# A convolution kernel's last stage keeps four row blocks on chip and scatters them to the output

## The chip, the cores and the metric

The kernel runs on one core of one Trainium2 chip. The metric is the device time of one execution in microseconds (us), the median of several executions. A profiled execution leaves a trace of every instruction and every DMA packet, and that is what is read here. Engine names are those of the profile: PE is the matrix engine (its weight loads are listed as PEld), DVE the vector engine, ACT the scalar engine, POOL the GpSimd engine and SP the sync engine, which here only issues transfers.

## The reference

The input x is one picture of 512 x 512 places with 64 channels in float32 (67.1 MB). Two layers follow each other, each adding its result to x:

```
x = x + L0(_gn(x), sequence_mask, ...)   # 0/1 mask over the 512 places; its drawn pattern is data
x = x + L1(_gn(x), w_real, w_imag)       # 12 x 12 Fourier modes, mixed over channels
return x

L0: xn = layer_norm(x)
    left  = (xn @ left_w  + left_b)  * mask * sigmoid(xn @ lgate_w + lgate_b)
    right = (xn @ right_w + right_b) * mask * sigmoid(xn @ rgate_w + rgate_b)
    out   = einsum('bkjd,bkid->bijd', left, right)
    out   = (layer_norm(out) @ out_w + out_b) * sigmoid(xn @ ogate_w + ogate_b)
L1: x_ft  = fft2(x)[:, :, :12, :12]
    out   = real(ifft2(einsum('bcmn,comn->bomn', x_ft, w)))
```

`_gn` is a group norm over the whole picture with 32 groups of 2 channels. So each layer needs statistics of all of its input before it can finish, and the second layer also needs the 12 x 12 low Fourier modes of all of it. The value of a place after the second layer is the value after the first plus an inverse transform of 12 x 12 modes.

## The kernel before

**Ranks.** About half of the 512 mask entries are not zero, and `mask[k] * mask[j]` makes the product of the first layer vanish elsewhere. At its start (L72 to L132) the kernel computes on chip a rank for each row: rows with mask come first. `hot` (L116) marks with ones where the rank of a row equals a slot; a matmul with it turns a table of row numbers and Fourier basis values into rank order (`slot_t`, L120 to L126). From that come `src_i`, the row numbers by rank, used by all gathers of x, and `dst_i` (L819), the ranks by row, used by the gathers of the last stage. The part with few masked rows (`compact`, L622 on) is the one that runs here.

**Stages.** The picture is cut into 16 column tiles of 32 columns (`JC`, `NJ`), and each of these into 4 blocks `b` of 128 rows. A column tile of one row block is 128 partitions x 8 KB, 1 MB; it is called a tile below. (1) to about 202 us: all 64 tiles of x are gathered in rank order, their statistics are taken, and masked entries are kept on chip; `group_norm_affine` (L253 to L280) makes the factors of the first group norm. (2) and (3): projections, then the product per channel. (4) from about 690 us: 8 short units for the product, and from about 800 us 32 units of two tiles each (`units`: column tile `jc`, half of the row blocks). A unit is gathered, gated and added, its group norm statistics and row transform are taken, and it is stored to scratch in DRAM (`store`, L1061, tensors `x1_h`), rows in rank order. A unit lies in one of five places on chip (`x_of`). The last unit pair is column tile 15. (5) the last stage, from about 1500 us: group norm, mixing of the modes over channels (`mixed_ps`, L1298), an inverse transform along columns for 128 columns at a time (`back_columns`, L1316 to L1348, which fills a quarter of `parts`), and then for each tile four matmuls with the row basis `rinv` (L1364), four additions on DVE onto the tile (L1371), and a store to the output (L1372, SP's queue).

**What sets the order in stage 5.** Tiles are handled in the order of `tiles_left`. There are 15 buffers (`AHEAD`). `fetch_rows(i)` gathers tile i from `x1_h` in the original row order by an indirect DMA on POOL's queue (L632) into buffer i mod 15; three are issued during the last units, twelve after them (L1250 to L1256), and each later one after the store of the tile that had the buffer. An instruction that has to wait holds up all that stand behind it on its engine's queue, the DMA issues too. `back_columns(0)` comes before tile 0, and `back_columns(1)`, `(2)` and `(3)` after tiles 4, 20 and 36:

```
for jc in range(NJ):
    for b in range(4):
        ...
        ahead = 4 * jc + b + AHEAD
        if ahead < len(tiles_left):
            fetch_rows(ahead)
        if jc % 4 == 1 and b == 0 and jc // 4 < 3:
            back_columns(jc // 4 + 1, pq, pt, False)
```

Tile names of the profile: `places` is the large region on chip that holds the five unit places, the mode weights and some of the buffers; `lx_t` are the other buffers; `x_h` is `x1_h`; `out_x` is the output.

Of the kernel before, what the change touches and what calls it, by code (L numbers as in the profile page):

```python
# [17 lines left out]
P = 128  # L18
# [11 lines left out]
JC = 32  # L30
NJ = N // JC
K = 2 * P
AHEAD = 15
# [13 lines left out]
def conv_preact_kernel(ctx: ExitStack, tc: tile.TileContext, t: dict):  # L47
# [5 lines left out]
    x1_d = dram.tile([N, N, C], F32, name="x1_d")  # L53
    x1_h = [dram.tile([N, HALF, C], F32, name=f"x1_h{h}") for h in range(2)]
    fwd_d = dram.tile([M2, N, C], F32, name="fwd_d")
    inv_d = dram.tile([M2, N, C], F32, name="inv_d")

    mask_i32 = const.tile([P, 4], I32, name="mask_i32")
    for b in range(4):
        nc.sync.dma_start(mask_i32[:, b : b + 1], t["sequence_mask"][:, b * P : (b + 1) * P].rearrange("o p -> p o"))  # L60

    def load_const(name, shape):
        c = const.tile(shape, F32, name=name)
        nc.scalar.dma_start(c, t[name])
        return c

    ident = load_const("c_ident", [P, P])
    center = load_const("c_center", [P, P])
    avg_p = load_const("c_avg_p", [P, P])
    avg_c = load_const("c_avg_c", [P, P])  # L70
    avg_h = load_const("c_avg_h", [P, 2])
    pick = load_const("c_pick", [P, G])  # L72


# [3 lines left out]
    src_i = const.tile([P, 4, NJ], I32, name="src_i")  # L78
    few_i = const.tile([P, NJ // 2], F32, name="few_i")
    nc.sync.dma_start(few_i, t["c_iota"][:, : NJ // 2])  # L80
    n_i = const.tile([1, 1], I32, name="n_i")
    with tc.tile_pool(name="ix", bufs=1) as xp, tc.tile_pool(
        name="ixp", bufs=1, space=PSUM
    ) as xps, tc.manual_schedule():

        def load_here(name, shape):
            c = xp.tile(shape, F32, name=name)
            nc.sync.dma_start(c, t[name])
# [6 lines left out]
        nc.vector.tensor_copy(table[:, :, 1], mask_i32)  # L95
# [18 lines left out]
        hot = xp.tile([P, 4, N], F32, name="hot")  # L114
        for b in range(4):
            nc.vector.tensor_scalar(hot[:, b, :], iota, rank_p[:, b : b + 1], None, ALU.is_equal)  # L116
        for sb in range(4):
            slot_ps = xps.tile([P, 2 + M2], F32, name="slot_ps", bufs=2)
            for b in range(4):
                nc.tensor.matmul(  # L120
                    slot_ps, hot[:, b, sb * P : (sb + 1) * P], table[:, b, :], start=(b == 0), stop=(b == 3)
                )
            nc.vector.tensor_copy(slot_t[:, sb], slot_ps)
            base = xp.tile([P, 1], F32, name="base", bufs=2)
            nc.vector.tensor_scalar(base, slot_t[:, sb, 0:1], float(NJ), None, ALU.mult)
            nc.vector.tensor_scalar(src_i[:, sb, :], iota[:, :NJ], base, None, ALU.add)  # L126
# [489 lines left out]
    def compact(fc):  # L616
# [31 lines left out]
        with tc.tile_pool(name="xc", bufs=1) as cp:  # L648
            xc = cp.tile([P, K + 1, 2, C], F32, name="xc")
            with tc.tile_pool(name="f1", bufs=1) as sp, tc.tile_pool(name="f1x", bufs=2) as xp, tc.tile_pool(  # L650
# [20 lines left out]
                for jc in range(NJ):  # L671
# [138 lines left out]
        with tc.tile_pool(name="tri", bufs=1) as trp:  # L810
# [3 lines left out]

            dst_i = fc.tile([P, 4, NJ // 2], I32, name="dst_i")
            base = fc.tile([P, 4], F32, name="dst_base")
            nc.vector.tensor_scalar(base, rank_p, float(NJ // 2), None, ALU.mult)
            for b in range(4):
# [49 lines left out]
            with tc.manual_schedule(), tc.tile_pool(name="late", bufs=1) as lp:  # L868
# [16 lines left out]
                def place(i):  # L885
                    return places[:, i * 64 * C : (i + 1) * 64 * C].rearrange("p (n c) -> p n c", c=C)
# [35 lines left out]
                ranked = [h.rearrange("s (k j) c -> (s k) (j c)", k=NJ // 2) for h in x1_h]  # L922
                tiles_left = [(jc, b) for jc in range(NJ) for b in range(4)]
                fetched = {}

                def fetch_rows(i):
                    jc, b = tiles_left[i]
                    fetched[jc, b] = buffers[i % AHEAD]
                    gather(fetched[jc, b].rearrange("p j c -> p (j c)"), ranked[jc // 8], dst_i, b, jc % 8)

# [3 lines left out]
                with tc.tile_pool(name="np_x", bufs=LEAD + 2) as tp, tc.tile_pool(  # L934
# [123 lines left out]
                    def store(k, r):  # L1058
                        jc, half = units[k]
                        b = 2 * half + r  # L1060
                        nc.sync.dma_start(  # L1061
                            x1_h[jc // 8][b * P : (b + 1) * P, (jc % 8) * JC : (jc % 8 + 1) * JC, :].rearrange("p j c -> p (j c)"),
                            x_of(k)[:, r * JC : (r + 1) * JC].rearrange("p j c -> p (j c)"),
                        )
# [59 lines left out]
                    for s in range(-LEAD, total_g + 2 * SIZE):  # L1124
# [115 lines left out]
                with tc.tile_pool(name="lq", bufs=1) as qp, tc.tile_pool(name="lx0", bufs=1) as xp0, tc.tile_pool(  # L1240
# [6 lines left out]
                    for i, xp in enumerate(xps):  # L1247
                        buffers += [xp.tile([P, JC, C], F32, name=f"lx_t{i}_{j}") for j in range((2, 2, 1)[i])]
                        if i > 0:
                            buffers += [place(i - 1)[:, r * JC : (r + 1) * JC] for r in range(2)]  # L1250
                    spare = places[:, 7 * 64 * C - 8 * 2 * MODES * M2 : 7 * 64 * C]
                    buffers += [spare[:, i * JC * C : (i + 1) * JC * C].rearrange("p (n c) -> p n c", c=C) for i in range(2)]
                    for i in range(len(fetched), AHEAD):
                        if i == 8:
                            nc.gpsimd.memset(picks, 0.0)
                        fetch_rows(i)  # L1256
                    pick4 = qp.tile([P, 4], F32, name="pick4")
                    nc.scalar.dma_start(pick4, t["c_pick4"])
# [4 lines left out]
                    with tc.tile_pool(name="sps", bufs=1, space=PSUM) as sps:  # L1263
# [85 lines left out]
                    with tc.tile_pool(name="lpq0", bufs=4, space=PSUM) as pq, tc.tile_pool(  # L1349
                        name="lpt0", bufs=4, space=PSUM  # L1350
                    ) as pt:
                        back_columns(0, pq, pt, True)
                    with tc.tile_pool(name="lpq", bufs=2, space=PSUM) as pq, tc.tile_pool(
                        name="lpt", bufs=2, space=PSUM
                    ) as pt, tc.tile_pool(name="lps", bufs=4, space=PSUM) as pp:
                        for jc in range(NJ):
                            for b in range(4):
                                it = parts[:, jc // 8, (jc % 8) * N : (jc % 8 + 1) * N]
                                xt = fetched.pop((jc, b))
                                group = []  # L1360
                                for g in range(4):
                                    ps = pp.tile([P, JC, 16], F32, name="l_ps")
                                    h = slice(32 * g, 32 * g + M2)
                                    nc.tensor.matmul(  # L1364
                                        ps.rearrange("p j o -> p (j o)"), rinv[h, b, :], it[h],
                                        start=True, stop=True, tile_position=(32 * g, 0),
                                    )
                                    group.append(ps)
                                for g, ps in enumerate(group):
                                    os_ = slice(16 * g, 16 * g + 16)  # L1370
                                    nc.vector.tensor_add(xt[:, :, os_], xt[:, :, os_], ps)  # L1371
                                nc.sync.dma_start(  # L1372
                                    out[0, b * P : (b + 1) * P, jc * JC : (jc + 1) * JC, :].rearrange("i j c -> i (j c)"),
                                    xt.rearrange("p j c -> p (j c)"),
                                )
# [82 lines left out]
```

## Time and profile before

| what | before |
|---|---|
| device time, median of 3 (range) | 1820.17 us (1819.5 to 1820.96) |
| device time of the profiled execution | 1827.94 us |
| span of its trace | 1826.1 us |
| busy: PE, DVE, ACT, POOL | 90%, 78%, 53%, 52% of the span |
| moved by DMA | 467.94 MB, mean 256 GB/s |
| HBM read, written | 278.05 MB, 187.56 MB |

The span runs from the first to the last instruction or landing of the trace; 1.84 us of the device time lie around it. The profiled execution took 7.8 us (0.43%) longer than the median of the others. Busy shares are means over stages with quite different limits. A waiting instruction is listed with what released it, and idle time of an engine counts only where that engine is on the way to the end.

### The profile page before, as it was taken

The page shows a single profiled execution, that of the slowest core. Times are in us where ns is not written, and L with a number is a line of the kernel's source. Part 1 is how long each engine was busy: PE and PEld are TensorE (multiplying, and loading weights), DVE is VectorE, ACT ScalarE, POOL GpSimd, SP SyncE. Part 2 cuts the span into 40 slices and gives each one's busy share as a digit, 9 for nine tenths or more (in the row PEclk, how much of TensorE's full clock was granted, in tenths as well). Part 3 has the DMA queues.
Part 4 walks back from the last instruction along what each step waited for, and adds up shares of the span by engine and source line. Part 5 has one row for each costly group of instructions (what it writes and reads, how often), then busy time and mean ns, then how long its engine had stood idle before and what let it go on. Part 6 is the DMA issues. An engine that isn't in the chain of part 4 may idle for free. (4 is left out here: it accounts for less than half of the span.)

```text
span 1826.1 us, 33612 instructions
## 1 busy us (share of the span) xinstructions
PE 1643.6 (90%) x11414; PEld 1290.0 (71%) x11414; DVE 1422.8 (78%) x2968; ACT 961.5 (53%) x1708; POOL 945.0 (52%) x711
## 2 busy tenths in 40 slices
PE   6779899999899999998999999999999967998772
PEld 5666666665687878897888888888888844665431
DVE  6989777777555547888999999999999996765542
ACT  3565565554222249986777777777777751111000
POOL 3656211111000005788999999999999892211120
PEclk9989899999899999999999999999999986555555
DMA  6999245555655512576866776777668689999999
GB/s 253 386 385 370 102 124 137 137 138 149 203 184 175 183 58 117 197 275 237 274 238 243 258 254 229 252 268 271 241 228 291 218 251 414 423 427 426 427 427 382
DMA packets 189573, 467.94 MB, mean 256 GB/s; under 512 B 34896, under 2 KB 134224, under 8 KB 148432
## 3 DMA queue, kind: packets, MB, share of 16 engines
q1 hardware_dynamic: 158496, 262.21, 42.4%
q0 software_dynamic: 27712, 201.40, 28.7%
q10 hardware_dynamic: 3184, 2.08, 0.4%
q8 instruction: 93, 1.52, 0.3%
q14 instruction: 88, 0.72, 0.1%
HBM read 278.05 MB, written 187.56 MB: 255 GB/s over the span
## 5 line engine op out<-in xcount | busy, mean ns | idle before, releaser
L982 PE MATMUL w_ps<-gate_x,xt_c 128*128 128x128 f32 x2048 | 280.6, 281 | 30.3 <-DVE z_t L1198 24.8
L1045 POOL TENSOR_TENSOR places<-places,z_t 128x1024 f32<-128x1024 f32 x127 | 301.0, 2370 | 8.0
L982 PEld LDWEIGHTS w_ps<-gate_x,xt_c 128*128 128x128 f32 x2048 | 252.5, 194 | 45.5 <-DVE z_t L1198 40.5
L982 PE MATMUL c_ps<-center_x,xt_c 128*128 128x128 f32 x2048 | 277.4, 279 | 1.3 <-ACT xt_c L1011 0.7
L982 PEld LDWEIGHTS c_ps<-center_x,xt_c 128*128 128x128 f32 x2048 | 253.6, 195 | 4.0 <-ACT xt_c L977 2.1
L1364 PE MATMUL l_ps<-places,rinv 24*128 24x512 f32 x512 | 207.8, 1125 | 28.5 <-DVE places L1371 18.5
L1100 DVE BATCH_NORM_STATS2 stats2c<-places 128x6 f32<-128x128 f32 x1024 | 220.6, 279 | 8.0 <-POOL places L1045 8.0
L1015 DVE TENSOR_REDUCE scratch<-sq_c 128x16 f32<-128x1024 f32 x160 | 194.6, 1216 | 29.6 <-ACT sq_c L1010 18.6
L1202 POOL TENSOR_TENSOR z_t<-z_t,bias_row_out 128x1024 f32<-128x1024 f32 x32 | 75.6, 2364 | 248.5 <-DVE z_t L1198 244.4
L1149 ACT ACTIVATE z_t<-z_t 128x1024 f32<-128x1024 f32 x128 | 135.4, 1058 | 129.1 <-DVE z_t L1204 111.5
L972 PE MATMUL t_ps<-c_ident,places 128*128 128x128 f32 x1280 | 200.4, 280 | 1.3 <-DVE places L857 1.3
L1364 PEld LDWEIGHTS l_ps<-places,rinv 24*128 24x128 f32 x512 | 120.5, 303 | 110.9 <-DVE places L1371 57.2
L972 PEld LDWEIGHTS t_ps<-c_ident,places 128*128 128x128 f32 x1280 | 145.7, 142 | 61.6 <-issue 53.9
L977 ACT ACTIVATE xt_c<-t_ps,ab_xc 128x512 f32<-128x512 f32 x256 | 176.0, 688 | 14.7 <-PE t_ps L972 13.6
L1198 DVE TENSOR_TENSOR z_t<-w_ps,rs_n 128x512 f32<-128x512 f32 x256 | 172.1, 672 | 9.8 <-PE w_ps L982 9.7
L1007 ACT ACTIVATE sq_c<-c_ps 128x512 f32<-128x512 f32 x256 | 150.5, 588 | 32.8 <-PE c_ps L982 31.3
L682 DVE BATCH_NORM_STATS2 stats1c<-x_ps 128x6 f32<-128x512 f32 x256 | 156.1, 683 | 11.7 <-PE x_ps L681 11.2
L1204 DVE TENSOR_TENSOR z_t<-z_t,scratch 128x1024 f32<-128x1024 f32 x128 | 156.3, 1221 | 9.9 <-ACT rs_n L1021 3.7
L1041 POOL TENSOR_TENSOR z_t<-z_t,places 128x1024 f32<-128x1024 f32 x64 | 151.5, 2367 | 14.7 <-ACT z_t L1149 14.6
L1041 POOL TENSOR_TENSOR z_t<-z_t,bias_row_out 128x1024 f32<-128x1024 f32 x63 | 149.2, 2368 | 5.7 <-ACT z_t L1149 5.4
L1371 DVE TENSOR_TENSOR places<-places,l_ps 128x512 f32<-128x512 f32 x176 | 109.5, 683 | 54.7 <-DMA places<-x_h,dst_i 43.6
L736 POOL COPY rbc<-rq_out 128x512 f32<-128x512 f32 x64 | 38.3, 613 | 212.4 <-DVE rq_out L209 132.0
(211 smaller groups left out, 2749.1 us busy)
## 6 DMA issues: line engine op xcount, KB each, us to landing
x_h<-places SPq DMA_DIRECT2D x64, 1024.0 KB
out_x<-places SPq DMA_DIRECT2D x44, 1024.0 KB
places<-u_d SPq DMA_DIRECT2D x512, 64.0 KB
out_x<-lx_t SPq DMA_DIRECT2D x20, 1024.0 KB
left_d<-o_c SPq DMA_DIRECT2D x64, 256.0 KB
right_d<-o_c SPq DMA_DIRECT2D x64, 256.0 KB
left_raw<-left_d SPq DMA_DIRECT2D x64, 256.0 KB
right_raw<-right_d SPq DMA_DIRECT2D x64, 256.0 KB
```

The lines of the kernel that those rows point to most:

```text
L682: nc.vector.bn_stats(stats[:, 0, 16 * (jc % quarter) + 4 * r + c, :], ps.rearrange("p i k -> p (i k)"))
L972: nc.tensor.transpose(tps[:, i, :], flat[:, o : o + P], ident)
L977: nc.scalar.activation(xts[s], tps, AF.Identity, bias=ab1[:, 2:3])
L982: nc.tensor.matmul(ps[:, 2 * i : 2 * i + 2, :], xts[s][:, i, :], w, start=True, stop=True)
L1007: nc.scalar.activation(sq, cps, AF.Square)
L1015: nc.vector.tensor_reduce(totals[k % 2][:, 8 * (n - 1) : 8 * (n + 1)], sqs.pop(s // 2), AX.X, ALU.add)
L1041: nc.gpsimd.tensor_mul(zs[k, c], zs[k, c], u)
L1045: nc.gpsimd.tensor_add(xr, xr, zs.pop((k, c)))
L1100: nc.vector.bn_stats(st[k // 4][:, g, k % 4, :], x_of(k)[:, :, 2 * g : 2 * g + 2])
L1198: nc.vector.tensor_mul(z[:, 8 * odd : 8 * odd + 8, :], wps, rs)
L1204: nc.vector.tensor_add(z, z, bias_ps["ogate"].unsqueeze(1).to_broadcast([P, 16, C]))
L1364: nc.tensor.matmul(ps.rearrange("p j o -> p (j o)"), rinv[h, b, :], it[h], start=True, stop=True, tile_position=(32 * g, 0),)
```

## The change

The change has five parts.

1. **Column tile 15 is not stored and not gathered.** Its two units stay where they lie (`place(order[0])`, `place(order[1])`) and become buffers 0 to 3. `tiles_left` begins with its four blocks, so the other 60 tiles follow as tiles 4 to 63, and eleven of them are gathered ahead. `x1_h` becomes three tensors of five column tiles.
2. **Their rows are in rank order.** A row basis in rank order, `rank_inv`, is made on chip: three ACT operations spread `hb` to `by_slot`, four transposes on PE between the variance matmul and the mixing, one ACT copy. The four finished tiles are stored by indirect DMAs on POOL's queue, each row to its own place in the output.
3. **`back_columns` in another order:** (3) first, then (0), (1) and (2) after tiles 0, 10 and 26.
4. **The ranks' chain:** the mask is loaded by one DMA, not four, the tables that the chain needs are issued first and on two queues, and `hot` is made for 128 slots at a time between the matmuls that use it.
5. **Matmuls whose result nobody reads** (`at_work`): four of 128x512 ahead of the first group norm's mean, one ahead of its reciprocal root.

```diff
-x1_h = [dram.tile([N, HALF, C], F32, name=f"x1_h{h}") for h in range(2)]
+x1_h = [dram.tile([N, PART * JC, C], F32, name=f"x1_h{h}") for h in range((NJ - 1) // PART)]
...
-for b in range(4):
-    nc.sync.dma_start(mask_i32[:, b : b + 1], t["sequence_mask"][:, b * P : (b + 1) * P].rearrange("o p -> p o"))
+nc.sync.dma_start(mask_i32, t["sequence_mask"].rearrange("o (b p) -> p (o b)", p=P))
...
-tri = load_here("c_tri", [P, P])
-ones = load_here("c_ones", [P, P])
-iota = load_here("c_iota", [P, N])
-table = load_here("c_table", [P, 4, 2 + M2])
+table = load_here(nc.scalar, "c_table", [P, 4, 2 + M2])
+tri = load_here(nc.sync, "c_tri", [P, P])
+ones = load_here(nc.scalar, "c_ones", [P, P])
+iota = load_here(nc.sync, "c_iota", [P, N])
...
-for b in range(4):
-    nc.vector.tensor_scalar(hot[:, b, :], iota, rank_p[:, b : b + 1], None, ALU.is_equal)
+def mark(sb):
+    for b in range(4):
+        one = slice(sb * P, (sb + 1) * P)
+        nc.vector.tensor_scalar(hot[:, b, one], iota[:, one], rank_p[:, b : b + 1], None, ALU.is_equal)
+mark(0)
 for sb in range(4):
...
+    if sb < 3:
+        mark(sb + 1)
...
-ab1 = group_norm_affine(fc, sets, 2 * stats.shape[2], "xc")
+def at_work(count):
+    ps = pt.tile([P, 4, P], F32, name="x_ps")
+    for _ in range(count):
+        nc.tensor.matmul(ps, ident, flat[:, : 4 * P], start=True, stop=True)
+at_work(4)
+ab1 = group_norm_affine(fc, sets, 2 * stats.shape[2], "xc", with_variance=lambda ab: at_work(1))
...
-buffers = [place(7)[:, JC:], places[:, free : free + JC * C].rearrange("p (n c) -> p n c", c=C)]
+buffers = [place(i)[:, r * JC : (r + 1) * JC] for i in order[:2] for r in range(2)]
+buffers += [place(7)[:, JC:], places[:, free : free + JC * C].rearrange("p (n c) -> p n c", c=C)]
...
-tiles_left = [(jc, b) for jc in range(NJ) for b in range(4)]
-fetched = {}
+tiles_left = [(jc, b) for jc in (NJ - 1, *range(NJ - 1)) for b in range(4)]
+fetched = {(NJ - 1, b): buffers[b] for b in range(4)}
...
-if n == 7 and held(0) and v < last:
+if n == 7 and held(0) and v < last - 1:
     store(v, 0)
-if n == 3 and held(1) and v - 1 < last:
+if n == 3 and held(1) and v - 1 < last - 1:
     store(v - 1, 1)
-if n == 6 and v - 1 == last:
-    for r in range(2):
-        store(last, r)
...
+by_slot = places[:, 7 * 64 * C : 7 * 64 * C + 4 * P].rearrange("p (b g m) -> p b g m", b=4, g=4)
+rank_inv = places[:, 7 * 64 * C + 4 * P : 7 * 64 * C + 8 * P].rearrange("p (b k) -> p b k", b=4)
+for k, factor in enumerate((1.0, -1.0)):
+    nc.scalar.mul(by_slot[:, :, :, k:M2:2], hb[:, :, k:M2:2].unsqueeze(2).to_broadcast([P, 4, 4, MODES]), factor / (N * N))
+nc.scalar.copy(by_slot[:, :, :, M2:], hb[:, :, M2:].unsqueeze(2).to_broadcast([P, 4, 4, 32 - M2]))
...
+turned_b = ps_t.tile([P, 4, P], F32, name="t_ps")
+for b in range(4):
+    nc.tensor.transpose(turned_b[:, b, :], by_slot[:, b].rearrange("p g m -> p (g m)"), ident)
+nc.scalar.copy(rank_inv, turned_b)
...
-back_columns(0, pq, pt, True)
+back_columns(3, pq, pt, True)
...
-for jc in range(NJ):
-    for b in range(4):
+for i, (jc, b) in enumerate(tiles_left):
+        kept = jc == NJ - 1
...
-ps.rearrange("p j o -> p (j o)"), rinv[h, b, :], it[h],
+ps.rearrange("p j o -> p (j o)"), (rank_inv if kept else rinv)[h, b, :], it[h],
...
+if kept:
+    nc.gpsimd.indirect_dma_start(
+        out=out.rearrange("o h (k j) c -> (o h k) (j c)", k=NJ),
+        out_offset=bass.IndirectOffsetOnAxis(ap=src_i[:, b, jc : jc + 1], axis=0),
+        in_=xt.rearrange("p j c -> p (j c)"), in_offset=None,
+    )
+else:
     nc.sync.dma_start(
...
-ahead = 4 * jc + b + AHEAD
+ahead = i + AHEAD
 if ahead < len(tiles_left):
     fetch_rows(ahead)
-if jc % 4 == 1 and b == 0 and jc // 4 < 3:
-    back_columns(jc // 4 + 1, pq, pt, False)
+if i in (0, 10, 26):
+    back_columns(i // 10, pq, pt, False)
```

More of the change, by code (lines that the diff above doesn't have):

```diff
@@ L31 @@
 NJ = N // JC
+PART = 5
 K = 2 * P
@@ L65, in load_const @@
         return c
[L67 to L72, printed above, removed]
     rank_p = const.tile([P, 4], F32, name="rank_p")
@@ L78, in conv_preact_kernel @@
     src_i = const.tile([P, 4, NJ], I32, name="src_i")
-    few_i = const.tile([P, NJ // 2], F32, name="few_i")
-    nc.sync.dma_start(few_i, t["c_iota"][:, : NJ // 2])
+    few_i = const.tile([P, PART], F32, name="few_i")
     n_i = const.tile([1, 1], I32, name="n_i")
@@ L84, in conv_preact_kernel, with load_here @@
     ) as xps, tc.manual_schedule():
-        def load_here(name, shape):
+        def load_here(queue, name, shape):
             c = xp.tile(shape, F32, name=name)
-            nc.sync.dma_start(c, t[name])
+            queue.dma_start(c, t[name])
             return c
-        tri = load_here("c_tri", [P, P])
-        ones = load_here("c_ones", [P, P])
-        iota = load_here("c_iota", [P, N])
-        table = load_here("c_table", [P, 4, 2 + M2])
+        table = load_here(nc.scalar, "c_table", [P, 4, 2 + M2])
+        tri = load_here(nc.sync, "c_tri", [P, P])
+        ones = load_here(nc.scalar, "c_ones", [P, P])
+        iota = load_here(nc.sync, "c_iota", [P, N])
+        ident = load_const("c_ident", [P, P])
+        center = load_const("c_center", [P, P])
+        avg_p = load_const("c_avg_p", [P, P])
+        avg_c = load_const("c_avg_c", [P, P])
+        avg_h = load_const("c_avg_h", [P, 2])
+        pick = load_const("c_pick", [P, G])
+        nc.sync.dma_start(few_i, t["c_iota"][:, :PART])
         nc.vector.tensor_copy(table[:, :, 1], mask_i32)
@@ L813, in compact @@
             tri = places.rearrange("p (j r c) -> p j r c", r=2, c=C)
-            dst_i = fc.tile([P, 4, NJ // 2], I32, name="dst_i")
+            dst_i = fc.tile([P, 4, PART], I32, name="dst_i")
             base = fc.tile([P, 4], F32, name="dst_base")
-            nc.vector.tensor_scalar(base, rank_p, float(NJ // 2), None, ALU.mult)
+            nc.vector.tensor_scalar(base, rank_p, float(PART), None, ALU.mult)
             for b in range(4):
@@ L919, in compact @@
                 free = 3 * 64 * C + C * MODES * MODES
-                buffers = [place(7)[:, JC:], places[:, free : free + JC * C].rearrange("p (n c) -> p n c", c=C)]
+                buffers = [place(i)[:, r * JC : (r + 1) * JC] for i in order[:2] for r in range(2)]
+                buffers += [place(7)[:, JC:], places[:, free : free + JC * C].rearrange("p (n c) -> p n c", c=C)]
                 buffers += [place(2)[:, r * JC : (r + 1) * JC] for r in range(2)]
-                ranked = [h.rearrange("s (k j) c -> (s k) (j c)", k=NJ // 2) for h in x1_h]
-                tiles_left = [(jc, b) for jc in range(NJ) for b in range(4)]
-                fetched = {}
+                ranked = [h.rearrange("s (k j) c -> (s k) (j c)", k=PART) for h in x1_h]
+                tiles_left = [(jc, b) for jc in (NJ - 1, *range(NJ - 1)) for b in range(4)]
+                fetched = {(NJ - 1, b): buffers[b] for b in range(4)}
                 def fetch_rows(i):
@@ L928, in fetch_rows @@
                     fetched[jc, b] = buffers[i % AHEAD]
-                    gather(fetched[jc, b].rearrange("p j c -> p (j c)"), ranked[jc // 8], dst_i, b, jc % 8)
+                    gather(fetched[jc, b].rearrange("p j c -> p (j c)"), ranked[jc // PART], dst_i, b, jc % PART)
                 ends = []
@@ L1061, in store @@
                         nc.sync.dma_start(
-                            x1_h[jc // 8][b * P : (b + 1) * P, (jc % 8) * JC : (jc % 8 + 1) * JC, :].rearrange("p j c -> p (j c)"),
+                            x1_h[jc // PART][b * P : (b + 1) * P, (jc % PART) * JC : (jc % PART + 1) * JC, :].rearrange("p j c -> p (j c)"),
                             x_of(k)[:, r * JC : (r + 1) * JC].rearrange("p j c -> p (j c)"),
@@ L1248, in compact @@
                         buffers += [xp.tile([P, JC, C], F32, name=f"lx_t{i}_{j}") for j in range((2, 2, 1)[i])]
-                        if i > 0:
-                            buffers += [place(i - 1)[:, r * JC : (r + 1) * JC] for r in range(2)]
                     spare = places[:, 7 * 64 * C - 8 * 2 * MODES * M2 : 7 * 64 * C]
@@ L1256, in compact @@
                         fetch_rows(i)
+                    by_slot = places[:, 7 * 64 * C : 7 * 64 * C + 4 * P].rearrange("p (b g m) -> p b g m", b=4, g=4)
+                    rank_inv = places[:, 7 * 64 * C + 4 * P : 7 * 64 * C + 8 * P].rearrange("p (b k) -> p b k", b=4)
+                    for k, factor in enumerate((1.0, -1.0)):
+                        nc.scalar.mul(
+                            by_slot[:, :, :, k:M2:2],
+                            hb[:, :, k:M2:2].unsqueeze(2).to_broadcast([P, 4, 4, MODES]), factor / (N * N),
+                        )
+                    nc.scalar.copy(by_slot[:, :, :, M2:], hb[:, :, M2:].unsqueeze(2).to_broadcast([P, 4, 4, 32 - M2]))
                     pick4 = qp.tile([P, 4], F32, name="pick4")
@@ L1371, in compact @@
                                     nc.vector.tensor_add(xt[:, :, os_], xt[:, :, os_], ps)
[L1372 to L1375, printed above, removed]
-                                ahead = 4 * jc + b + AHEAD
+                                if kept:
[3 more added lines that the diff above has]
+                                        in_=xt.rearrange("p j c -> p (j c)"), in_offset=None,
+                                    )
+                                else:
+                                    nc.sync.dma_start(
+                                        out[0, b * P : (b + 1) * P, jc * JC : (jc + 1) * JC, :].rearrange("i j c -> i (j c)"),
+                                        xt.rearrange("p j c -> p (j c)"),
+                                    )
+                                ahead = i + AHEAD
                                 if ahead < len(tiles_left):
                                     fetch_rows(ahead)
-                                if jc % 4 == 1 and b == 0 and jc // 4 < 3:
-                                    back_columns(jc // 4 + 1, pq, pt, False)
+                                if i in (0, 10, 26):
+                                    back_columns(i // 10, pq, pt, False)
     rows_with_mask = nc.values_load(n_i[0:1, 0:1], min_val=0, max_val=N)
```

## The prediction

> **What bounds the kernel now.** The first thing read was the page's strip of 40 slices:
>
> ```profile
> DMA  6999245555655512576866776777668689999999
> GB/s 253 386 385 370 102 124 137 137 138 149 203 184 175 183 58 117 197 275 237 274 238 243 258 254 229 252 268 271 241 228 291 218 251 414 423 427 426 427 427 382
> ```
>
> DMA is full in slices 2 to 4 (x is gathered) and from slice 34 on. Next, busy time by stretch over the end (columns: length, busy us of PE, PEld, DVE, ACT and POOL, granted PE clock, DMA share, GB/s):
>
> ```profile
> 1479.00:1539.40 60.40, 39.19 (x252) 23.94 (x253) 43.01 (x136) 18.02 (x38) 35.69 (x26) 0.74 1.01 361
> 1539.40:1821.60 282.20, 223.60 (x597) 136.16 (x594) 156.72 (x252) 20.03 (x36) 45.90 (x49) 0.50 1.01 424
> 22.00:195.00 173.00, 142.72 (x1011) 115.28 (x1009) 156.39 (x279) 102.64 (x341) 99.65 (x209) 0.96 0.98 381
> ```
>
> After 1539.4 us DMA at about 426 GB/s is the limit, and the end comes when all bytes are moved. Whether it is also the limit from 1479 to 1539.4 a share of 1.01 cannot tell, so the chain of waits was read there, with the timeline for SP's and POOL's transfers:
>
> ```profile
> 1519.13 6.96 PE mixed_ps L1298 x72
> ...
> 1534.64 1.02 ACT places L1348
> ...
> 1535.70 1.18 PE l_ps L1364 x8
> 1536.88 0.68 DVE places L1371
> ```
> ```profile
> 1539.37 8.88 SPq L1372 DMA_DIRECT2D out_x<-places  x4
> ...
> 1550.82 12.18 SPq L1372 DMA_DIRECT2D out_x<-lx_t  x2
> ```
> ```profile
> 1502.22 0.98 POOL L632 DMA_INDIRECT places<-x_h,dst_i  x1
> 1503.51 0.94 POOL L632 DMA_INDIRECT lx_t<-x_h,dst_i  x1 [0.30 <-issue]
> ...
> 1522.98 0.94 POOL L632 DMA_INDIRECT places<-x_h,dst_i  x1 [2.52 <-DMA lx_t<-x_h,dst_i]
> ...
> 1547.08 0.94 POOL L632 DMA_INDIRECT places<-x_h,dst_i  x1 [22.58 <-DVE places L1371]
> 1549.51 0.94 POOL L632 DMA_INDIRECT places<-x_h,dst_i  x1 [1.49 <-DVE lx_t L1371]
> 1551.93 0.93 POOL L632 DMA_INDIRECT places<-x_h,dst_i  x1 [1.48 <-DMA out_x<-places]
> 1557.45 0.94 POOL L632 DMA_INDIRECT places<-x_h,dst_i  x1 [4.59 <-DMA out_x<-places]
> ```
>
> What to see: from the mode mixing to the first finished tile the chain is PE, ACT and DVE, with no transfer in it. The first output store leaves at 1539.37; call that T0. Until then DMA works ahead (last stores to scratch, 15 gathers), stopping only where buffers run out. So T0 is set by computing, and the end by T0 plus what is left to move.
>
> One tile is 1.0486 MB, at 426 GB/s 2.46 us. Left at T0: 64 - 15 = 49 gathers and 64 stores, 113 x 2.46 = 278.0 us, and about 3.5 us of the last gathers ahead (issued to 1522.98), together 281.5. The stretch above took 282.2. The model holds, and the end is read by it.
>
> The start is a chain of its own:
>
> ```profile
> 7.63 0.17 DVE L95 CAST c_table<-mask_i 128x4 f32<-128x4 int32 x1 [7.63 <-DMA c_table<-in_c_table]
> 10.82 1.68 DVE L116 TENSOR_SCALAR hot<-c_iota,rank_p 128x512 f32<-128x512 f32 x4
> ...
> 14.24 1.08 POOL L632 DMA_INDIRECT xg<-in_x,src_i  x1 [13.78 <-DVE src_i L126]
> ```
>
> Nothing large moves before 14.24, and DMA is 0.98 busy from 22 to 195, so an earlier first gather moves everything after it.
>
> **The change, part by part.**
>
> *Ranks' chain.* DVE begins at 7.63, 2.7 us after the issue of the table (4.94), the last of nine transfers on SP. Now the table is ACT's first (0.75) and the mask SP's first (0.76). 0.75 + 2.7 = 3.5 is the early end; 1.8 us more, what issuing four mask loads took, is the late one, 5.3. I take 4.3: 3.3 us gained. `hot` for 128 slots: each operation shrinks from about 0.45 us to at most the 0.28 us of a 128x128 tensor-scalar on DVE (L806), and the matmuls hide part; 0.3. The later marks run under matmuls (four take about 1.7 us, four marks 1.1); uncovered they would cost 3 x 1.1. Sum **-3.6** (-2.0 to -4.5).
>
> *`at_work`.* Between 199.2 (last transpose) and 203.94 (mean) PE stands idle for DVE, and its clock falls:
>
> ```profile
> 204.00:214.20 10.20, 7.78 (x34) 7.06 (x35) 3.68 (x20) 2.82 (x4) 0.00 (x0) 0.50 0.00 0
> ```
>
> Four matmuls of two records each, 0.43 us apiece (L750's 0.589 for 512 columns against L681's 0.272 for 128 gives 0.83 ns a column), fill 3.4 us of that gap; without the gap they would delay the mean by as much. If the clock stays up, the rounds of `cc_ps` at the start of stage 2, 2.75 us then 1.85, save 0.9 each, three of them: -2.7. If it falls anyway, nothing; should the fifth matmul run into the first transposes, +0.5. I take half, **-1.3**. [...]
>
> *Before T0.* The three small ACT operations come while ACT waits for DVE (from 1511); the four transposes (8 records, about 2 us at the low clock) fall in the nine-step reciprocal root on DVE, 1516.0 to 1518.0, when PE has nothing, and the copy ends by about 1518, needed at 1535. Cost 0; without the cover some 3 us. Four scratch stores and four gathers go, 8 x 2.46 = 19.7 us of DMA. All eight lay before T0, which no transfer sets: gain 0 there. Buffers 0 to 3 now hold the kept tiles, so only eleven gathers can go ahead, and DMA will stand idle before T0.
>
> *After T0.* Left are again 49 gathers and 64 stores (four of them scatters): 113, as before. What remains of the 19.7 us is the 3.5 us backlog: **-3.5**. Against it stand three new waits, all at the front.
>
> (a) `back_columns(0)` now comes after tile 0. The same call after tile 4 before made the next store wait 1562.66 - 1550.82 = 11.8 us where the pitch is 2.85. So tile 1 is done at T0 + 11.8, tile 2 at 14.7, tile 3 at 17.5, tile 4 at 20.4.
>
> (b) On POOL's queue scatter and gather alternate, and each gather (15 to 18) needs the scatter just ahead to have left its buffer. From a store's issue to the gather that waits for it the trace has 1539.37 to 1547.08 = 7.7, then 7.3, 6.9, and 9.5 under more load. I take 7.0, as little else moves then, with 5.0 and 9.5 as ends.
>
> (c) In the changed kernel's list of instructions and waits, the first plain store (tile 4, L1404 there) waits for all four scatters, since these write rows of the output known only at run time. All of SP's stores stand behind it, and gathers 19 on behind those.
>
> By hand from T0: scatter 0 at 0.3, gather 15 at 7.3; scatter 1 at 12.1 (tile 1), gather 16 at 19.1; scatter 2 at 20.3 (1.25 per issue on POOL), behind gather 16 in its queue, 2 us more, so gather 17 at 29.3; scatter 3 at 30.6, landed about 38. First bytes of the plain stores at 39. In these 39 us seven tiles have moved, 17.2 us: **+21.8** idle (with the ends, 15.7 to 29). From there seven finished tiles wait and DMA stays full, also over `back_columns(1)`, now after tile 10.
>
> [...]
>
> *Sum:* -3.6 - 1.3 - 3.5 + 21.8 = +13.4 us. On the profiled execution 1827.94 + 13.4 = 1841.3; its 7.8 us above the median are not the change's, so 1820.2 + 13.4, rounded, **1833**.
>
> **Rivals.**
>
> *Faster: T0 is not the gate.* If computing before T0 secretly hangs on DMA (it is full from 1480), eight transfers less bring T0 forward by up to 19.7 us while the front costs less. For: share 1.01. Against: the chain above. It decides once T0 comes more than 13.4 us earlier; with all 19.7, 1820.2 + 13.4 - 19.7 = 1814. With the front's idle time hidden as well, 1820.2 - 19.7 - 4.9 = 1796.
>
> *The scatter wait costs little.* Should a scatter's turn take some 3 us, the four are over when tile 4 is done; the plain stores' first bytes come at 22, four tiles moved till then, 22 - 9.8 = 12 idle, from the pause of `back_columns(0)` alone: 1820.2 - 8.4 + 12 = 1824. For: nothing else uses DMA then. Against: no turn under 6.9 in the trace.
>
> *No change within 0.2%* (3.6 us, about what a measurement can tell): the start gains its bound, 7.2, and idle time is the least, 15.7: 1820.2 - 7.2 - 3.5 + 15.7 = 1825 is the closest the bounds come; a warm PE clock through `mixed_ps` (3.5 us of 6.96) would make it 1822.
>
> **How the numbers follow.** My forecast 0.66; the cheap wait 0.10, which is still slower; within 0.2% 0.07; faster 0.17. So faster 0.17, same 0.07, slower 0.76. The likeliest case alone spans 1825 to 1844 (idle 15.7 with the best start; idle 29 with the poorest: -2 + 0.5 - 3.5 + 29 = 24). Reaching towards the faster cases, the range is 1815 to 1844.
>
> **What the profile after would show.** Right: the first gather near 10.6; DMA idle from about 20 us before the first scatter, then two or three tenths dark up to the first plain store some 38 us after it; SP waiting there for a POOL transfer; POOL's gathers waiting for `out_x`. Clock 1.00 near 205 if `at_work` works. Wrong: the first l_ps much less than 34 us after the last statistics begin (1501 to 1535.7 now), or plain stores within 25 us of the first scatter.

## The result, and the profile after

The changed kernel takes **1832.45 us** (median of 7 runs, 1827.81 to 1834.90); the kernel before, beside it, 1821.49 us (7 runs, 1819.50 to 1824.37). The ratio is **1.0059** (95% interval 1.0048 to 1.0069): 11 us slower. Forecast were 1833 us and 1815 to 1844. A second comparison gave 1.0044 (1.0031 to 1.0058).

The profiled execution of the changed kernel took 1828.97 us, span 1827.2: low among its own runs, as that of before was high among its (1827.94). The two profiles alone show a difference of 1 us where the medians show 11. So for everything that follows a second profile of each is used as well, taken on one chip (below: *before_again*, *after_again*).

The start, from the timeline of the changed kernel (start, length in us, engine, line, operation, idle time before it and what ended it):

```profile
0.75 0.44 ACTq L80 DMA_DIRECT2D c_table<-in_c_table  x1
3.29 0.17 DVE L94 CAST c_table<-mask_i 128x4 f32<-128x4 int32 x1 [3.29 <-DMA mask_i<-in_sequence_mask]
7.15 1.66 DVE L118 TENSOR_SCALAR hot<-c_iota,rank_p 128x128 f32<-128x128 f32 x8
10.36 1.09 POOL L638 DMA_INDIRECT xg<-in_x,src_i  x1 [9.90 <-DVE hot L118]
```

DVE starts at 3.29 instead of 7.63, and the first gather leaves at 10.36 instead of 14.24.

The last stage, from the timeline too: the start of the last statistics, the first matmuls of a kept tile, then every scatter (L1398) and gather (L638) on POOL's queue, and the first plain stores on SP's.

```profile
1485.84 4.34 DVE L1116 BATCH_NORM_STATS2 stats2c<-places 128x6 f32<-128x128 f32 x22
...
1519.00 2.09 PE L1389 MATMUL l_ps<-places 24*128 24x512 f32 x8 [1.10 <-ACT places L1373]
...
1523.87 1.00 POOL L1398 DMA_INDIRECT out_x<-places,src_i  x1 [22.86 <-DVE places L1396]
...
1530.23 0.96 POOL L638 DMA_INDIRECT places<-x_h,dst_i  x1 [5.36 <-DMA out_x<-places,src_i]
...
1535.18 0.99 POOL L1398 DMA_INDIRECT out_x<-places,src_i  x1 [3.99 <-DVE places L1396]
...
1540.53 0.96 POOL L638 DMA_INDIRECT places<-x_h,dst_i  x1 [4.35 <-DMA out_x<-places,src_i]
...
1541.79 0.98 POOL L1398 DMA_INDIRECT out_x<-places,src_i  x1 [0.30 <-DVE places L1396]
...
1549.99 0.96 POOL L638 DMA_INDIRECT places<-x_h,dst_i  x1 [7.22 <-DMA out_x<-places,src_i]
...
1551.26 0.98 POOL L1398 DMA_INDIRECT out_x<-places,src_i  x1 [0.30 <-issue]
...
1559.58 3.11 SPq L1404 DMA_DIRECT2D out_x<-places  x4
1559.65 0.96 POOL L638 DMA_INDIRECT places<-x_h,dst_i  x1 [7.41 <-DMA out_x<-places,src_i]
```

Every gather here is released by a scatter's landing, and the first plain store, of a tile whose buffer four DVE additions had finished at about 1543.5, leaves only at 1559.58. The view of waits, for SP's queue from 1520 us on (engine, line, what it waited for: total us, times, longest), names the cause:

```profile
SPq L1404 <- DMA out_x<-places: 133.2, 30, 4.9
SPq L1404 <- DMA out_x<-places,src_i: 78.0, 1, 78.0
```

One wait of 78.0 us, for a scatter. It is counted from SP's instruction before, at about 1481.6; for the last 16 us of it a finished tile stood waiting, and four stores leave within 3.11 us behind it. What it costs in transfers stands in the table by stretch (length, busy us of PE, PEld, DVE, ACT and POOL, granted PE clock, DMA share, GB/s):

```profile
1500.00:1512.30 12.30, 7.22 (x78) 3.89 (x77) 5.12 (x21) 0.59 (x1) 1.01 (x3) 0.72 0.98 404
1512.30:1523.87 11.57, 7.81 (x50) 5.56 (x50) 6.14 (x11) 4.92 (x10) 0.00 (x0) 0.65 0.01 6
1523.87:1559.58 35.71, 34.10 (x112) 23.65 (x110) 23.86 (x39) 5.25 (x9) 6.84 (x7) 0.50 0.57 206
1559.58:1822.50 262.92, 196.21 (x483) 112.65 (x480) 132.44 (x214) 13.35 (x24) 43.20 (x46) 0.50 1.01 423
204.00:214.20 10.20, 8.88 (x66) 7.70 (x65) 3.28 (x8) 6.52 (x10) 0.00 (x0) 0.95 0.00 0
```

The eleven gathers ahead are through at 1512.3; for 11.6 us DMA has nothing. Then come 35.7 us in which it moves 206 GB/s, half of the 423 in the row behind. From 1559.58 on it is full to the end. The last row is the stretch of time that had clock 0.50 before: now 0.95. It does not hold quite the same work, since stage 2 begins 3.7 us earlier here (first `cc_ps` at 205.66, before at 209.34).

### The profile page after: what moved, and what is told of

Its sections match the earlier page's. It is cut to its first block, busy times and chain, and to the rows that moved or that the text cites. A ratio compares the mean times of both kernels' runs of the same rounds, so it can differ in the third digit from the quotient of the medians.

```text
span 1827.2 us, 33627 instructions
## 1 busy us (share of the span) xinstructions
PE 1647.5 (90%) x11428; PEld 1283.9 (70%) x11428; DVE 1423.7 (78%) x2980; ACT 962.8 (53%) x1712; POOL 946.5 (52%) x711
## 4 chain that ended last, share of the span: by engine, by line
PE 28%; DVE 17%; DMA 10%; POOL 3%; issue 2%; ACT 2%; SPq 1%; DVEq 0%; ACTq 0%; POOLq 0%
PE w_ps L998 6%; PE c_ps L998 6%; DMA places<-x_h,dst_i 5%; PE l_ps L1389 4%; PE t_ps L988 4%; DVE stats2c L1116 4%; DVE z_t L1214 4%; DVE scratch L1031 4%; PE y_ps L1009 4%; DVE z_t L1220 3%; DMA lx_t<-x_h,dst_i 3%; PE f_ps L1088 2%; POOL z_t L1057 1%; POOL places L1061 1%; DVE places L1396 1%
## 5 line engine op out<-in xcount | busy, mean ns | idle before, releaser
L998 PE MATMUL w_ps<-gate_x,xt_c 128*128 128x128 f32 x2048 | 278.9, 280 | 30.6 <-DVE z_t L1214 29.0
L1389 PEld LDWEIGHTS l_ps<-places,rinv 24*128 24x128 f32 x480 | 116.1, 306 | 119.9 <-DVE places L1396 63.5
L1057 POOL TENSOR_TENSOR z_t<-z_t,places 128x1024 f32<-128x1024 f32 x64 | 151.7, 2370 | 13.6 <-ACT z_t L1165 13.4
```

The costliest lines, as they stand in the source:

```text
L998: nc.tensor.matmul(ps[:, 2 * i : 2 * i + 2, :], xts[s][:, i, :], w, start=True, stop=True)
L1057: nc.gpsimd.tensor_mul(zs[k, c], zs[k, c], u)
L1389: nc.tensor.matmul(ps.rearrange("p j o -> p (j o)"), (rank_inv if kept else rinv)[h, b, :], it[h], start=True, stop=True, tile_position=(3 ...
```

## The experiments

Line numbers differ a little between the kernels below; L1398, L1385 (in *kept*) are the scatters, L638, L637, L633, L632 the gathers. The runs of the kernel before beside these kernels took 1825 to 1826 us, not 1821.5, so ratios are compared, not times. For each kernel's profiled execution four marks are read: when the first output store (or scatter) is issued, **T0**; when the first plain store is; when the last packet of the trace ends; and the **idle time**, the stretch from T0 to that last packet less the bytes moved in it at 426.3 GB/s, its rate where it is full. Packets that load code are left out of both.

| kernel | ratio to before (95% interval) | T0 | first plain store | T0 to last packet | bytes after T0 | idle |
|---|---|---|---|---|---|---|
| before, first profile | 1 | 1539.37 | T0 | 284.9 | 119.5 MB | 4.6 |
| before_again | 1.000 (0.9991 to 1.0009) | 1539.36 | T0 | 286.7 | 118.8 MB | 8.1 |
| after, first profile | 1.0059 (1.0048 to 1.0069) | 1523.87 | T0 + 35.7 | 301.8 | 118.5 MB | 23.9 |
| after_again | 1.0044 (1.0031 to 1.0058) | 1530.47 | T0 + 33.7 | 300.0 | 118.5 MB | 22.0 |
| head | 0.9964 (0.9951 to 0.9976) | 1532.03 | T0 | 285.2 | 120.0 MB | 3.8 |
| kept | 1.0079 (1.0065 to 1.0093) | 1538.54 | T0 + 33.8 | 299.6 | 118.5 MB | 21.7 |
| pause | 1.0056 (1.0043 to 1.0069) | 1529.31 | T0 + 33.2 | 299.6 | 118.5 MB | 21.6 |
| plain | 0.9993 (0.9984 to 1.0001) | 1531.05 | T0 | 290.2 | 118.5 MB | 12.2 |
| group | 1.0035 (1.0021 to 1.0049) | 1532.65 | T0 + 24.9 | 298.3 | 118.5 MB | 20.4 |
| both | 1.0015 (1.0006 to 1.0024) | 1530.42 | T0 + 20.8 | 293.4 | 118.5 MB | 15.5 |
| plain_pause | 0.9975 (0.9963 to 0.9987) | 1529.51 | T0 | 287.5 | 118.5 MB | 9.6 |
| last | 1.006 (1.0042 to 1.0078) | 1527.60 | T0 | 297.6 | 118.5 MB | 19.7 |

The theory was that T0 is set by computing, that parts 4 and 5 bring it forward, and that the scatters' waits after T0 cost more. The main rival: transfers set T0, and the eight that are gone bring it forward.

### head: the kernel before with parts 4 and 5 alone

The edit, cut to its core:

```diff
+nc.sync.dma_start(mask_i32, t["sequence_mask"].rearrange("o (b p) -> p (o b)", p=P))
+table = load_here(nc.scalar, "c_table", [P, 4, 2 + M2])
...
+mark(0)
...
+at_work(4)
+ab1 = group_norm_affine(fc, sets, 2 * stats.shape[2], "xc", with_variance=lambda ab: at_work(1))
```

> The kernel before with parts 4 and 5 alone (the ranks' chain and the matmuls whose result nobody reads); last stage as before. My theory: the first gather leaves at 10.4 instead of 14.24 us, the first group norm's factors and stage 2 gain 1.3 more, nothing else moves: 4 to 6 us less than before, 1821.5 - 5 = 1816.5, and the first output store comes some 5 us earlier too. Rival, the gain is lost on the way (some later stage waits for a transfer that has not moved): within 0.1% of before, 1821.

Measured: 1820.09 us (5 runs) against 1826.11, ratio 0.9964, 6.0 us by the medians. The first gather leaves at 9.73, and the first output store 7.3 us earlier than in either profile of before; the stretch behind it is as long as before (285.2 us). Nothing of the gain is lost on the way, and the time is at the upper end of the 4 to 6 us expected. This kernel is faster than both.

### kept: the changed kernel without parts 4 and 5

```diff
-at_work(4)
-ab1 = group_norm_affine(fc, sets, 2 * stats.shape[2], "xc", with_variance=lambda ab: at_work(1))
+ab1 = group_norm_affine(fc, sets, 2 * stats.shape[2], "xc")
```

The loads, `hot` and the ranks' chain are those of before as well.

> The changed kernel without parts 4 and 5: only the four kept tiles, their row basis and the order of back_columns. My theory: the first scatter leaves when the first output store left before (give or take 2 us), and the tail behind it is longer by 17 to 18 us: 1821.5 + 17 = 1838 (1835 to 1841). Rival, transfers gated the first output: of the 15.5 us by which the first output came earlier in the profile after, only about 5.5 are parts 4 and 5, and the other 10 are the eight transfers that are gone; then this kernel's first scatter comes 10 us earlier and the time is 1821.5 - 10 + 17 = 1828.

Measured: ratio 1.0079, 15.6 us by the medians (1841.74 against 1826.11). Its timeline on POOL's queue:

```profile
1538.54 1.00 POOL L1385 DMA_INDIRECT out_x<-places,src_i  x1 [22.06 <-DVE places L1383]
1543.38 0.96 POOL L633 DMA_INDIRECT places<-x_h,dst_i  x1 [3.84 <-DMA out_x<-places,src_i]
...
1572.37 0.96 POOL L633 DMA_INDIRECT places<-x_h,dst_i  x1 [7.06 <-DMA out_x<-places,src_i]
```

T0 is 1538.54, within 1 us of before. Eight transfers less move T0 by less than 1 us in this execution; they did not gate it, and the rival, 10 us, falls. The tail is 13 to 15 us longer than in the two profiles of before, not 17 to 18. The two halves multiply to the whole: 0.9964 x 1.0079 = 1.0043, and after_again has 1.0044 (the first comparison 1.0059).

### before_again and after_again: both kernels once more, unchanged

> The kernel before once more, unchanged, for a second profile on the chip that also runs the changed one. Ratio 1.000; from the first output store to the last packet 285 us, as in the first profile (1539.37 to 1824.3). If the first profile's first output store (1539.37) was late by that execution's 7.8 us, it comes at 1530 to 1535 here.

> The changed kernel once more, unchanged. My theory: against the kernel before on the same chip the first output comes 5 to 7 us earlier and the tail from it to the last packet is 15 to 17 us longer, together 10 to 11 us slower. Rival: the first output comes some 15 us earlier, as in the first pair of profiles, because transfers gated it; then the tail must be longer by 26 us, which the first profile (301.9 against 284.9) does not have.

Measured: 1825.87 (ratio 1.000) and 1834.45 us (1.0044). T0 of before is 1539.36 again; I had thought it late by that execution's 7.8 us; but the first profile's 1827.94 us agrees with the runs of before on this chip (1825.87), not with those of 1821.5 us. T0 of after_again is 1530.47, 8.9 us earlier than before_again, not 15.5 as in the first pair. Laying the DVE and POOL instructions of the first pair side by side, in order, shows most of why: besides the start (3.9 us) and stage 2 (1.4) the offset jumps by 3.7 us between 421 and 673 us and by 4.1 at about 860 us, in code that the change does not touch. In the second pair the same two places lose 1.3 us and gain 1.4. So jumps of this size belong to the execution. After_again's tail is 13.2 us longer than before_again's; the first pair's, 16.9. Expected were a T0 5 to 7 us earlier and a tail 15 to 17 us longer: both miss, in directions that make up for each other in part. The rival (15 us and 26 us) falls.

### plain: the four kept tiles by plain stores

```diff
-if kept:
-    nc.gpsimd.indirect_dma_start(out=..., out_offset=bass.IndirectOffsetOnAxis(ap=src_i[:, b, jc : jc + 1], axis=0), ...)
-else:
-    nc.sync.dma_start(out[0, b * P : (b + 1) * P, ...], xt)
+nc.sync.dma_start(out[0, b * P : (b + 1) * P, ...], xt)
```

> The changed kernel with the four kept tiles stored by plain stores on SP's queue, as all others are. Left out: their rows stay in rank order, so these rows of the output are in other places than the reference's. This takes away the scatters' alternation with the gathers on POOL's queue and the plain stores' wait for all scatters, and leaves the pause after tile 0. My theory: idle time of DMA after the first output falls from 18.5 us to about 7 (12 us of pause less two tiles): 10 to 12 us less than the changed kernel, 1821. Rival, the scatters' waits cost little and the pause is the price: within 3 us of the changed kernel, 1830.

Measured: ratio 0.9993. After_again lies at 1.0044; the difference of 0.0051 is 9 us (0.0066, 12 us, against the first ratio). The tail is 290.2 us, 10 to 12 less than with scatters, and idle time 12.2 instead of 22 to 24. The scatters' waits are more than half of the price; the rival, that they cost little, falls. Idle time of 12.2 is 5 more than forecast: the idle time that before has too (4.6, some 2.8 of it from 1820 to 1824.3 us, where its DMA share falls from 0.81 to 0.08) was not in that estimate.

### pause, group and both: the two new causes of idle time, singly and together

*Pause*:

```diff
-if i in (0, 10, 26):
+if i in (3, 10, 26):
     back_columns(i // 10, pq, pt, False)
```

*Group*:

```diff
-ahead = i + AHEAD
-if ahead < len(tiles_left):
-    fetch_rows(ahead)
+for ahead in [] if i < 3 else range(AHEAD, AHEAD + 4) if i == 3 else [i + AHEAD]:
+    if ahead < len(tiles_left):
+        fetch_rows(ahead)
```

*Both*: the two edits together.

> The changed kernel with back_columns(0) after the fourth kept tile instead of after the first, so that the four kept tiles are done 2.85 us apart. My theory: the chain of scatter and gather on POOL's queue takes most of the time by itself; the scatters are issued at about 0, 7.6, 15 and 24 us after the first (0, 11.3, 17.9, 27.4 in the changed kernel), and the first plain store comes at about 32 instead of 35.7: 3 to 4 us less than the changed kernel, 1829. Rival, the pause of back_columns sets the idle time: the first plain store comes as soon as tile 4 is done, at about 20, and the time is 12 to 15 us less, 1819.

> The changed kernel with gathers 15 to 18 behind all four scatters on POOL's queue; back_columns(0) still after tile 0. My theory: the last scatter leaves when tile 3 is done, 17 us after the first, not 27; the first plain store comes at about 25 instead of 35.7 us; until then four scatters and two gathers move (14.8 us), idle 10 instead of 18.5: 8 us less than the changed kernel, some 3 us above the kernel before. Rival, the order on POOL's queue does not matter: the time of the changed kernel, 11 us above the kernel before.

> The changed kernel with both moves: gathers 15 to 18 behind the four scatters, and back_columns(0) after the fourth kept tile. My theory: scatters at 0, 2.9, 5.7 and 8.6 us, gathers 15 to 18 from 9.8 on, while tile 4 waits for back_columns(0) until 20.4; by then eight tiles have moved (19.7 us), so the idle time falls from 18.5 to 1 to 4 us: 15 to 17 us less than the changed kernel, 4 to 7 us under the kernel before, level with parts 4 and 5 alone or up to 3 us better (the backlog of 3.5 us is gone). Rival, each move gives only what it gives alone: 10 us less than the changed kernel, the time of the kernel before.

Measured: *pause* 1.0056 and a first plain store at T0 + 33.2: only 0.5 to 2.5 us earlier, its tail 0.4 to 2.2 shorter. The 3 to 4 us that I expected do not show in the time (the changed kernel has 1.0044 and 1.0059). The rival, 12 to 15 us, falls: with the pause moved, the queue's alternation fills the time by itself. *Group* 1.0035, about 1 us by the medians below after_again where 8 were expected, and *both* 1.0015, 5.6 us where 15 to 17 were: both misses. *Group* can hardly be told from its rival, that the order on POOL's queue does not matter. The timeline of *both* on POOL's queue shows what I had left out:

```profile
1530.42 1.00 POOL L1398 DMA_INDIRECT out_x<-places,src_i  x1 [22.86 <-DVE places L1396]
1535.80 0.97 POOL L1398 DMA_INDIRECT out_x<-places,src_i  x1 [4.38 <-DVE places L1396]
1541.15 0.96 POOL L1398 DMA_INDIRECT out_x<-places,src_i  x1 [4.38 <-issue]
1546.50 0.96 POOL L1398 DMA_INDIRECT out_x<-places,src_i  x1 [4.39 <-DMA out_x<-places,src_i]
1547.77 0.98 POOL L638 DMA_INDIRECT places<-x_h,dst_i  x1 [0.30 <-issue]
```

The scatters do not leave when their tiles are done (2.85 us apart) but 5.35 us apart, and the releaser of the last one is named: the scatter before it. Each writes rows of the output that are known only at run time, and each waits for the one ahead, as the first plain store does. In the changed kernel this is not seen, since there a gather between two scatters waits for the same landing. Of 5.35 us, 2.46 are a tile's transfer at full rate; nearly 3 us a scatter are lost where no other work runs beside them.

### plain_pause: no scatter, and the pause behind the kept tiles

The edit of *plain*, and in addition:

```diff
-if i in (0, 10, 26):
+if i in (3, 10, 26):
     back_columns(i // 10, pq, pt, False)
```

> The kernel with plain stores for the four kept tiles (their rows stay in rank order, so these rows of the output are in other places than the reference's), and back_columns(0) after the fourth kept tile. No scatter is left, and the pause comes when four stores and four gathers can run in it. My theory, that the scatters' waits on one another and the plain stores' wait for them are all that is left of the price: idle time of DMA after the first output falls to 3 to 6 us, the tail to 281 to 284 us (286 in the kernel before), and the time is 7 to 10 us under the kernel before, ratio 0.995. Rival, some idle time belongs to the eleven instead of fifteen tiles gathered ahead and stays: tail 288 or more, ratio 0.999.

Measured: ratio 0.9975, tail 287.5, idle time 9.6. This lies between the two, nearer to the rival by the tail. With scatters and pause both out of the way the front still has a few us more idle time than *head* (3.8). What keeps them wasn't taken apart; the two candidates, eleven tiles ahead instead of fifteen and the place of the pause, stay open. What is shown: even without a single scatter, keeping the four tiles did not shorten the tail (287.5 against 285.2 in *head*).

### last: the kept tiles at the end of the list

```diff
-tiles_left = [(jc, b) for jc in (NJ - 1, *range(NJ - 1)) for b in range(4)]
+tiles_left = [(jc, b) for jc in range(NJ) for b in range(4)]
...
-fetched[jc, b] = buffers[i % AHEAD]
+fetched[jc, b] = buffers[4 + i % (AHEAD - 4)]
...
-back_columns(3, pq, pt, True)
+back_columns(0, pq, pt, True)
...
-ahead = i + AHEAD
-if ahead < len(tiles_left):
+ahead = i + AHEAD - 4
+if ahead < len(tiles_left) - 4:
     fetch_rows(ahead)
-if i in (0, 10, 26):
-    back_columns(i // 10, pq, pt, False)
+if i in (4, 20, 36):
+    back_columns(i // 16 + 1, pq, pt, False)
```

> The changed kernel with the four kept tiles handled last, the gathered tiles in eleven buffers, back_columns in the order of the kernel before. The front is that of the kernel before, and the scatters come behind all plain stores. My theory: each scatter waits for the one before it, 5.35 us a turn of which 2.46 is transfer, and the first waits for the landing of the last plain store, some 4 us: tail 278 - 3.5 to 0 of backlog, + 4 + 4 x 2.9 + 2 = 292 to 297 us, first output 7 to 9 us earlier, ratio 0.999 to 1.002. Rival, at the end of the queue the scatters cost nothing more than their transfers: tail 281, ratio 0.993, better than parts 4 and 5 alone (0.9964).

Measured: ratio 1.006, no better than at the front. The end of this kernel in the table by stretch (columns as above):

```profile
1780.00:1800.00 20.00, 16.29 (x40) 9.93 (x40) 14.91 (x24) 0.00 (x0) 0.00 (x0) 0.50 0.99 417
1800.00:1804.00 4.00, 0.00 (x0) 0.00 (x0) 0.00 (x0) 0.00 (x0) 0.00 (x0) 0.50 0.18 72
1804.00:1810.00 6.00, 0.00 (x0) 0.00 (x0) 0.00 (x0) 0.00 (x0) 0.99 (x1) 0.50 0.43 178
```

And its scatters in the timeline on POOL's queue:

```profile
1804.82 0.99 POOL L1398 DMA_INDIRECT out_x<-places,src_i  x1 [36.13 <-DMA out_x<-lx_t]
1810.21 0.97 POOL L1398 DMA_INDIRECT out_x<-places,src_i  x1 [4.40 <-DMA out_x<-places,src_i]
1815.58 0.96 POOL L1398 DMA_INDIRECT out_x<-places,src_i  x1 [4.39 <-DMA out_x<-places,src_i]
1820.88 0.96 POOL L1398 DMA_INDIRECT out_x<-places,src_i  x1 [4.34 <-issue]
```

The first scatter now waits for the last plain store's landing (POOL has been idle for 36.1 us then), and each other one for the one before: pitch 5.3 to 5.4 us with DMA at 0.43. The mechanism is as expected, the size above it: 1.006 where 0.999 to 1.002 was expected. The tail of 297.6 us is just past the upper end, and the span (1831.4) ends 6.2 us after the last packet, where the other kernels need 1.3 to 1.8. That rest is not the last scatter's landing, which SP has seen at 1825.77. By the trace it is a DRAIN at the end of POOL's queue, from 1823.22 to 1830.54. Every kernel here has one behind its last indirect transfer, 7.3 to 14.9 us long; in the others it is over 26 us before the span ends. What it waits for is not shown. The rival (scatters at no more than their transfers, 0.993) falls.

## Why the prediction was right

The time came out as forecast, and mainly for the reason forecast. That 1833 lies within 1 us of 1832.45 is in part luck. The four terms as measured below, -4.3, -1.2, -2.2 and +17.0, make +9.3 instead of +13.4, and the forecast was added to 1820.2, while the kernel before took 1821.5 beside the changed one. Point by point:

- **T0 plus what is left to move.** Right. Behind the first plain store DMA is nearly full to the end in every kernel with the scatters in front (423 GB/s in the changed one), and *head*, whose T0 moved with an unchanged tail, moved its time with it (T0 -7.3, time -6.0).
- **The rival that T0 hangs on DMA.** Excluded by *kept*: T0 moved by 0.8 us. In the first pair of profiles alone (15.5 us earlier) it would have looked true.
- **Ranks' chain, -3.6 (-2.0 to -4.5).** The first gather leaves at 9.68 to 10.65 us in the nine executions with part 4 that were read (mean 9.95), at 14.21 to 14.30 in three without: -4.3. The term was slightly too small because DVE starts at 3.3, below the early end of 3.5 (the releaser is now the mask; the table, issued first, no longer is). The 0.3 us for `hot` do not show: from DVE's start to the first gather it takes 6.6 us with part 4 and without.
- **`at_work`, -1.3 (+0.5 to -2.7).** From the start of the `set_mean` reduction, at the end of stage 1, to the thirtieth reduction behind it on DVE it takes 91.8 to 92.1 us in three executions without, 89.8 to 91.8 in nine with it (means 91.96 and 90.76): -1.2. The half that I took is a mean over executions that differ. After_again kept its clock (granted from 205 to 208 us: 1.00), *head*, with the same code up to here, lost it (0.50). The same matmuls of stage 2 in the timeline on PE, first of after_again:

```profile
205.18 1.16 PE L733 MATMUL cc_ps<-c_center,gc_t 128*128 128x128 f32 x8 [1.01 <-ACT gc_t L726]
```

and then of *head*, at little over half the speed:

```profile
205.00 2.07 PE L732 MATMUL cc_ps<-c_center,gc_t 128*128 128x128 f32 x8
```

In *both*, too, the granted clock is 0.50 from 205 to 208 us. Why the clock holds in one execution and falls in another no run shows.

- **Before T0: 0.** *Kept* has T0 0.8 us earlier. Right, as far as one execution shows. In the profiles, though, T0 moved by more than the start explains. It is 1523.87 to 1532.65 in the nine executions with parts 4 and 5 (mean 1529.7) and 1538.54 to 1539.37 in the three without (mean 1539.1). That is 9.4 us, of which the start and stage 2 explain 5.5. The rest comes up in code that is the same, and its cause stays open; a part may be that before_again's profiled execution was 3.8 us slower than its median.
- **The backlog, -3.5.** Bytes after T0 are 118.5 MB in every kernel with kept tiles and 118.8 to 120.0 MB in three executions without: 0.3 to 1.5 MB, 0.7 to 3.5 us, mean 2.2. Somewhat too large.
- **Idle time after T0, +21.8 (15.7 to 29).** Measured 21.7 to 23.9 in the changed kernel and *kept*, 3.8 to 8.1 without kept tiles: +17.0. The order of events was right, the size too large. By the timeline of the changed kernel, from T0 (its additions end at 1523.6):

| step | by hand | measured |
|---|---|---|
| gather 15 | 7.3 | 6.6 |
| scatter 1, gather 16 | 12.1, 19.1 | 11.6, 16.9 |
| scatter 2, gather 17 | 20.3, 29.3 | 18.2, 26.4 |
| scatter 3 | 30.6 | 27.7 |
| first plain store | 38 | 36.0 |

The mis-sized term is **a scatter's turn, "I take 7.0"**. With nothing else on DMA it took 4.8 to 6.4 us for the first and 5.3 to 5.4 for the others; behind a gather in its queue 8.1 to 8.4, where 9.0 was used. My rows (6.9 to 9.5) came from stores on a full DMA (share 1.01).

The turns of 4.8 to 8.4 us run from issue to issue, so they include POOL's own issue, 0.96 to 1.0 us.

- **What sets the scatters.** Step (b) had them bound to the gathers between them. *Group* and *both* show that they are bound to one another as well; the prediction did not say so, and it did not matter for this order of the queue.
- **Sum.** Predicted -4.9 and +18.3. Measured: -6.0 for *head*, and a tail longer by 14.9 (mean of after, after_again and *kept*, 300.5, against 285.6 for the three without): +8.9, where the two timed comparisons have +11.0 and +8.5.
- **What the profile after would show.** The wait of SP, the gathers waiting for `out_x`, the matmuls of `l_ps` 33.2 us behind the start of the last statistics (34.6 before) and the first plain store (35.7 us after the first scatter, forecast 38) were right. DMA went dark 11.6 us ahead of the first scatter, not 20, and was half empty after it, not two or three tenths dark, which the forecast's own seven tiles in 39 us (0.44 busy) did not fit either.

## What to carry to other kernels

In these kernels an indirect store whose rows are known only at run time was ordered against the stores to the same tensor ahead of it and behind it, other indirect ones included (turns of 5.3 to 5.4 us in *both* and *last*; waits of 78.0 us by a plain store for a scatter, 36.1 us by a scatter for a plain store, both counted from the instruction ahead on their queue). Where that is so, count its landing, not its transfer, once for each of them, and look at what stands behind it on both queues. The transfers that were saved ahead of T0, which computing sets, saved next to nothing (0.8 us in *kept*, 2.2 by the bytes left after T0); here the gain lay in the start, and parts 4 and 5 alone (ratio 0.9964) are the version to keep. Where two profiles and the medians of many runs disagree, as here by 10 us, take each profile again before reading a gain out of a stage.

## What the runs showed that was not expected

- Successive scatters of 1 MB with nothing else on DMA leave 5.35 us apart, of which 2.46 are a tile's transfer at full rate and 0.96 to 1.0 the issue on POOL.
- POOL's queue ends with a DRAIN of 7.3 to 14.9 us behind the last indirect transfer; with the scatters at the end (*last*) it ends 4.8 us after SP has seen the last landing.
- Stages shifted by 4 us between two executions in code that is the same (jumps of 3.7 and 4.1 us at 421 to 673 and at 860 us), and one pair of profiles moved T0 by 15.5 us where another pair moved it by 8.9.
- Whether five extra matmuls keep the clock up changes from one execution to the next, with the same code up to there: 1.16 to 2.08 us for the same eight records of `cc_ps`, at a granted clock from 205 to 208 us of 1.00 in after_again and 0.50 in *head*.
